# Token parts, first weight pieces and output weights moved ahead at the seam between attention and FFN

## The chip, the cores and the metric

The kernel runs on one core of a Trainium2 chip. The metric is the device time in microseconds (us) of one execution; with several runs of a kernel, their median. Engines are called as the profile calls them: PE (TensorE, matmuls), PEld (its weight loads), DVE (VectorE), ACT (ScalarE), POOL (GpSimd), and SP (SyncE, which issues every DMA here). Each engine works through its own list of instructions in order and waits on semaphores for the others.

## The reference

A transformer block with both branches fed by one layer norm:

```
xn  = layernorm(x)                       # x: 1 x 2048 x 512, f32
qkv = xn @ w_qkv.T                       # 16 heads of 32
p   = softmax(causal(q k^T / sqrt(32)))
a   = (p v) @ w_o.T
gate, up = xn @ Wg.T, xn @ Wu.T          # Wg, Wu: 4096 x 512, Wd: 512 x 4096
inter    = gelu_tanh(gate) * up          # weights: 4-bit codes times a scale for 32 of them
out = x + a + inter @ Wd.T
```

## The kernel before

The order of the instructions on every engine is the order in which the program writes them (`manual_schedule`); pools of tiles decide which earlier reader a new tile has to wait for.

**Attention.** The 2048 tokens are four blocks `b` of 512, taken in `ORDER = (1, 2, 3, 0)`; the normalized tokens stand transposed in `xnT[b]`, 128 features by 512 tokens for each `k` of 4. Heads go in eight pairs `p`. A first part normalizes the tokens and makes values, queries and keys; its tiles for `x`, `wv` and `xn` live in pools of their own. A pair takes 40 steps, one for each block of queries `qb` and tile of keys `kt`. In a step `score_cols` starts two score tiles in PSUM with the negated row maxima (L281), `add_scores` adds the products (L296), `exponentials` turns them into probabilities on ACT (L310; on the diagonal, the last four `kt` of a block, L316 to L320 and POOL's affine select L321), and `attend` multiplies the step before by the values and by ones for the row sums (L344). When a block of queries is full, `keep_attention` copies the result on ACT (L363) and the sums on DVE (L364), and four `normalize_attention` follow, one for each step: a reciprocal on DVE (L372) and a product on POOL (L374). The last two pairs, with no row maxima left to find, run together in one loop of 40 steps. Score tiles rotate through three PSUM banks for each of two pools, and one step takes two of each.

**Output projection.** It starts with the loads of `w_o` (`wo`, L714) into buffers of the pool `gu`, and 16 loads of `x` into accumulators `acc` (L719), between which `fetch` loads three weight pieces. Then come 16 tiles of 128 tokens `n`, each with four matmuls into a PSUM bank `po` (L726), and DVE adds it to `acc` (L733). Eight banks take turns, here and in the FFN.

**Token parts.** The FFN's products are made from parts of 12 bits. For each `xnT[b][:, k]`, `token_rest` makes on DVE `high` (tile `highx`, L692), on POOL the rest `low` (tile `lm`, L693), and, one tile of the projection later, on DVE `mixed` (L695) and on ACT the rescaled `low` (L698). `token_high` makes `xh` on DVE (L703), in the buffer of an attention output that the projection has read. In the projection there is one `token_rest` for each tile `n`, 16 in all.

**Weight pieces.** `begin_piece` decodes 128 x 512 codes: five instructions on DVE (L582 to L596) and two on POOL (L602 or L608). `end_piece` cuts them: `high` on DVE (L620), two on ACT (L632, L633), two on POOL (L634, L635). For the down weights `raise_low` comes later on ACT (L645). Three pieces are made within the projection, and the fourth within the first unit of the FFN.

**FFN.** 128 units (g, j, b). A unit has 16 matmuls for gate and up (`high_and_low`, L765), each sum scaled in place on ACT (L772), four more for each (`mixed`, L778), the gelu on ACT (L797), the product `inter` on DVE (L801), and its parts (L805, L808, L809). The down product of a unit, `down`, is a generator which the next unit drives through `finish`: between gelu and up's `mixed` it makes the third part (L816), eight matmuls (L826) and four scalings on ACT (L833), and at the unit's end four matmuls (L838) and the sums into `acc` (L847).

Of the kernel before, what the change touches and what calls it, by code (L numbers as in the profile page):

```python
# [45 lines left out]
P = 128  # L46
# [29 lines left out]
def block_kernel(  # L76
# [11 lines left out]

    late = ctx.enter_context(tc.tile_pool(name="late", bufs=1, side="right"))
# [13 lines left out]
    with (  # L103
# [3 lines left out]
        tc.tile_pool(name="wa", bufs=2) as wa,  # L107
        tc.tile_pool(name="vals", bufs=1) as vals,
        tc.tile_pool(name="qk", bufs=10) as qkp,
# [4 lines left out]
        tc.tile_pool(name="clip", bufs=2) as clipp,  # L114
        tc.tile_pool(name="ps_s", bufs=3, space=PSUM) as ps_s,
# [261 lines left out]
        with (  # L377
            tc.tile_pool(name="x", bufs=1) as xp,
            tc.tile_pool(name="xn", bufs=2) as xnp,
        ):  # L380
            xs = []
            for t in range(NT):
                xt = xp.tile([P, H], F32, tag=f"x{t % 8}", name=f"x{t}")
                nc.sync.dma_start(out=xt, in_=x[t * P : (t + 1) * P, :])
                xs.append(xt)
                if t == 3:
                    wqk[0] = load_qk(0)
                    wv = xp.tile([P, NK, H], F32, tag="wv", name="wv")
                    nc.sync.dma_start(out=wv, in_=w_v.rearrange("p (k o) -> p k o", k=NK))
            wqk[1] = load_qk(1)  # L390
            mvs, rstds = {}, {}

            def statistics(b, first=0, n=4):
                key = f"{b}_{first}"
                mv = small.tile([P, n, 2], F32, tag="mv", name=f"mv{key}")
                for i in range(n):
                    st = small.tile([P, 6], F32, tag="st", name=f"st{key}_{i}")
                    nc.vector.bn_stats(st, xs[4 * b + first + i])
                    nc.vector.bn_aggr(mv[:, i, :], st)
                ve = small.tile([P, n], F32, tag="ve", name=f"ve{key}")  # L400
                nc.vector.tensor_scalar(ve, mv[:, :, 1], EPS, None, ALU.add)
                sd = small.tile([P, n], F32, tag="sd", name=f"sd{key}")
                nc.scalar.activation(sd, ve, AF.Sqrt)

                q = small.tile([P, n], F32, tag="q", name=f"q{key}")
                nc.vector.reciprocal(q, sd)
                nc.vector.tensor_tensor(q, q, ve, ALU.mult)
                nc.vector.tensor_tensor(q, q, sd, ALU.add)
                nc.vector.tensor_scalar(q, q, 0.5, None, ALU.mult)
                rstd = small.tile([P, n], F32, tag="rstd", name=f"rstd{key}")  # L410
                nc.vector.reciprocal(rstd, q)
                for i in range(n):
                    mvs[b, first + i], rstds[b, first + i] = mv[:, i, 0:1], rstd[:, i : i + 1]

            xns = {}

            def normalize(b, i):
                xn = xnp.tile([P, NK, 8, 16], F32, tag="xn", name=f"xn{b}_{i}")
                nc.vector.tensor_scalar(
                    xn,  # L420
                    xs[4 * b + i].rearrange("p (b r k) -> p k r b", b=16, r=8),
                    mvs[b, i],
                    rstds[b, i],
                    ALU.subtract,
                    ALU.mult,
                )
                xns[b, i] = xn

            def flip(b, i):

                bank = i % 2 if b == 0 else b < 3
                pt = ps_m.tile([P, TB], F32, tag=f"m{int(bank)}", name=f"ptx{b}_{i}")
                xn = xns.pop((b, i))
                for k in range(NK):
                    nc.tensor.transpose(  # L435
                        pt[:, k * P : (k + 1) * P], xn[:, k].rearrange("p r b -> p (r b)"), ident
                    )
                nc.scalar.copy(
                    xnT[b][:, :, i * P : (i + 1) * P],
                    pt.rearrange("p (k t) -> p k t", k=NK),  # L440
                )

            def value_halves(t):
                ps = ps_m.tile([P, H], F32, tag="m0", name=f"ps_v{t}")
                for k in range(NK):
                    nc.tensor.matmul(  # L446
                        ps,
                        lhsT=xnT[t // 4][:, k, (t % 4) * P : (t % 4 + 1) * P],
                        rhs=wv[:, k, :],
                        start=(k == 0),  # L450
                        stop=(k == NK - 1),
                    )
                    if k == 1:
                        yield
                nc.scalar.copy(v[t // 4][:, t % 4, :], ps)
                yield

            for i in range(4):
                if i % 2 == 0:
                    statistics(0, i, 2)  # L460
                normalize(0, i)
                flip(0, i)

            later = [(1, b, which) for b in range(NTB) for which in range(2)]
            for b in range(NTB):
                n = first[b]
                if b + 1 < NTB:
                    statistics(b + 1)
                    normalize(b + 1, 0)
                project(0, b, 0)  # L470
                project(0, b, 1)
                for i in range(4):
                    if b + 1 < NTB:
                        flip(b + 1, i)
                    full_width = [value_halves(4 * b + i)] * 2
                    if b >= 2:
                        full_width += [project_halves(*later.pop(0))] * 2
                    for j in range(b + 1):
                        rows_when_due()
                        tiles = [score_rows(0, n, ps_s), score_rows(1, n, ps_t)]  # L480
                        for p in range(2):
                            maxima(p, n, tiles[p])
                        if j == 0 and i < 3 and b + 1 < NTB:
                            normalize(b + 1, i + 1)
                        n += 1
                        for _ in range(-(-len(full_width) // (b + 1 - j))):
                            next(full_width.pop(0))
# [4 lines left out]
        for m in range((NP - 2) * STEPS):  # L492
# [25 lines left out]
            if og + 2 < NOG and own == 20:  # L518
                wqk[og + 2] = load_qk(og + 2)
        for n in range(STEPS):  # L520
            rows_when_due(joint=True)
            two = [score_cols(NP - 2, n, ps_t), score_cols(NP - 1, n, ps_s)]
            for i in range(2):
                add_scores(NP - 2 + i, n, two[i])
            for _ in range(2):
                attend(*pending.pop(0))
            for i in range(2):
                pending.append((NP - 2 + i, n, exponentials(NP - 2 + i, n, two[i])))
            while full:
                keep_attention()  # L530
            if invert:
                normalize_attention()
        while pending:
            attend(*pending.pop(0))
# [6 lines left out]
    lmp = ctx.enter_context(tc.tile_pool(name="lm", bufs=1, reuse_waits="tile"))  # L541
    accp = ctx.enter_context(tc.tile_pool(name="acc", bufs=1, reuse_waits="tile"))
    stage = ctx.enter_context(tc.tile_pool(name="stage", bufs=3, reuse_waits="tile"))
    tp = ctx.enter_context(tc.tile_pool(name="deq", bufs=2, reuse_waits="tile"))
    gup = ctx.enter_context(tc.tile_pool(name="gu", bufs=4, reuse_waits="tile"))
# [132 lines left out]


    lm = [lmp.tile([P, 2, NK, TB], F32R, tag=f"lm{b}", name=f"lm{b}") for b in range(NTB)]  # L680
    xh = {}

    def end(rest):
        if rest is not None:
            for _ in rest:
                pass

    def token_rest(b, k):

        x, low, mixed = xnT[b][:, k], lm[b][:, 0, k], lm[b][:, 1, k]  # L690
        high = tp.tile([P, TB], F32, tag="high", name=f"highx{b}_{k}")
        nc.vector.tensor_scalar(high.bitcast(I32), x.bitcast(I32), HIGH, None, ALU.bitwise_and)  # L692
        nc.gpsimd.tensor_tensor(low, x, high, ALU.subtract)  # L693
        yield
        nc.vector.scalar_tensor_tensor(  # L695
            mixed, high, SPLIT, low.bitcast(F32), ALU.mult, ALU.subtract
        )
        nc.scalar.activation(low, low.bitcast(F32), AF.Copy, scale=1.0 / SPLIT)  # L698
# [8 lines left out]
    with tc.manual_schedule():  # L707
# [10 lines left out]
        for n, t in enumerate(order):  # L718
            nc.sync.dma_start(out=acc[t], in_=x[t * P : (t + 1) * P, :])  # L719
            if n in (1, 2, 3):  # L720
                fetch()
        tokens = None
        for n, t in enumerate(order):
# [21 lines left out]
            if n in (3, 6, 9):  # L745
                begin_piece()
# [164 lines left out]
```

## Time and profile before

| | us |
|---|---|
| runs shown | 2002.93, 2003.64, 2005.29 |
| their median | 2003.64 |
| the profiled execution | 2003.17 |
| its span | 2001.5 |
| PE busy | 1954.4 |
| DVE busy | 1316.7 |
| ACT busy | 1105.0 |
| POOL busy | 730.8 |
| last two pairs of heads begin, about | 735 |
| first matmul of the output projection | 855.88 |
| its last one ends | 912.2 |
| third unit of the FFN begins | 940.95 |

All times of the profile come from one execution and are counted from the start of its span; the time of that execution is 1.67 us longer than the span. Rows of a stage give, after its length, the busy time of PE, PEld, DVE, ACT and POOL with the number of instructions, then the granted clock of PE (1.00 is full speed), the busy share of the DMA engines and GB/s. Rows of a timeline give start, length, engine, line, operation, output and input, and in brackets the idle time ahead of it with what ended it. A row of the chain gives start, length and what ran. A row of the waits reads "who <- for whom: us in total, times, the longest".

### The profile page before, as it was taken

To read this page: it belongs to the slowest core of one execution; us is meant where nothing else is said; L and a number is where in the kernel's file an instruction comes from. 1 tells how busy PE (TensorE), PEld (TensorE's weight loads), DVE (VectorE), ACT (ScalarE), POOL (GpSimd) and SP (SyncE) were. 2 spreads that over 40 slices of the span, in tenths; PEclk is the share of its full clock that TensorE was granted. 3 is DMA by queue.
4 is the path that set the end of the run, shared out by engine and by line. 5 is a ranking of instruction groups with operands and counts; after the bars stand their busy time and mean duration, and the time that the engine had idled before them with its cause. 6 is when DMAs were issued, how large, how long until landed. Compare 5 with 4: busy or idle time off the path is not lost.

```text
span 2001.5 us, 30992 instructions
## 1 busy us (share of the span) xinstructions
PE 1954.4 (98%) x11072; PEld 1162.7 (58%) x11072; DVE 1316.7 (66%) x2642; ACT 1105.0 (55%) x2360; POOL 730.8 (37%) x892
## 2 busy tenths in 40 slices
PE   7999999999999999997999999999999999999998
PEld 3433233333333322245888888888888888888886
DVE  5657665646565661178776767676767676767674
ACT  2112664546455667724666666666666666666664
POOL 1000110202111112155555555555555555555551
PEclk9999999999999999998999999999999999999999
DMA  3000000000000000030000000000000000000002
GB/s 126 0 11 11 1 2 1 1 1 1 1 1 1 1 2 1 1 128 17 24 22 19 22 20 21 20 22 19 22 19 22 19 21 20 22 19 22 19 6 84
DMA packets 54955, 39.79 MB, mean 20 GB/s; under 512 B 14736, under 2 KB 47504, under 8 KB 54672
## 3 DMA queue, kind: packets, MB, share of 16 engines
q1 hardware_dynamic: 54800, 37.81, 6.4%
q8 instruction: 87, 1.43, 0.3%
q14 instruction: 68, 0.56, 0.1%
HBM read 33.55 MB, written 4.19 MB: 19 GB/s over the span
## 4 chain that ended last, share of the span: by engine, by line
PE 93%; DVE 2%; ACT 2%; issue 1%; POOL 1%; DMA 0%; POOLq 0%; DVEq 0%; ACTq 0%
PE gu L765 23%; PE av L344 12%; PE pd L826 12%; PE gu L778 12%; PE ps_s L207 9%; PE ps_qk L163 6%; PE pd L838 6%; PE ps_t L281 4%; PE ps_t L296 3%; PE ps_v L446 3%; ACT prob L310 1%; PE po L726 1%; POOL lm L693 1%; PE pm L262 1%; PE ptx L435 0%
## 5 line engine op out<-in xcount | busy, mean ns | idle before, releaser
L765 PE MATMUL gu<-xh,gu 128*128 128x512 f32 x1024 | 403.3, 394 | 0.0
L765 PE MATMUL gu<-lm,gu 128*128 128x512 f32 x1024 | 399.9, 390 | 0.0
L231 DVE TENSOR_REDUCE tops<-ps_s 128x1 f32<-128x512 f32 x384 | 243.6, 681 | 157.5 <-PE ps_s L207 137.2
L847 DVE SCALAR_TENSOR_TENSOR acc<-pd,acc 128x512 f32<-128x512 f32 x512 | 316.7, 679 | 0.7 <-PE pd L838 0.7
L344 PE MATMUL av<-prob,v 128*32 128x512 f32 (+3 forms) x1280 | 288.8, 539 | 3.7 <-DVE sums L364 2.8
L310 ACT ACTIVATE prob<-ps_t 128x512 f32<-128x512 f32 x384 | 205.8, 597 | 154.5 <-PE ps_t L296 153.2
L207 PE MATMUL ps_s<-qk,qk 32*128 32x512 f32 (+3 forms) x1280 | 291.1, 576 | 0.0
L778 PE MATMUL gu<-lm,gu 128*128 128x512 f32 x1024 | 279.5, 395 | 10.3 <-ACT gu L772 10.3
L344 PE MATMUL av<-prob,ones 128*32 128x512 f32 (+3 forms) x1280 | 288.8, 539 | 0.0
L809 POOL TENSOR_TENSOR parts<-inter,hi 128x512 fp32r<-128x512 f32 x128 | 171.7, 1341 | 269.6 <-DVE hi L805 267.5
L801 DVE SCALAR_TENSOR_TENSOR inter<-gu,gate 128x512 f32<-128x512 f32 x128 | 88.5, 692 | 271.1 <-PE gu L778 266.8
L833 ACT ACTIVATE pd<-pd 128x512 f32<-128x512 f32 x512 | 263.2, 581 | 1.9 <-PE pd L826 1.9
L296 PE MATMUL ps_t<-qk,qk 32*128 32x512 f32 (+3 forms) x1280 | 263.6, 535 | 0.0
L826 PE MATMUL pd<-wd,parts 128*128 128x512 f32 x1024 | 260.5, 396 | 2.4 <-ACT parts L808 1.1
L772 ACT ACTIVATE gu<-gu 128x512 f32<-128x512 f32 x256 | 148.5, 580 | 182.8 <-PE gu L765 182.8
L778 PEld LDWEIGHTS gu<-lm,gu 128*128 128x128 f32 x1024 | 192.9, 188 | 56.6 <-ACT gu L772 10.7
L826 PEld LDWEIGHTS pd<-wd,parts 128*128 128x128 f32 x1024 | 192.6, 188 | 49.5 <-ACT parts L808 1.5
L765 PEld LDWEIGHTS gu<-xh,gu 128*128 128x128 f32 x1024 | 192.7, 188 | 46.5 <-ACT lm L698 0.2
L765 PEld LDWEIGHTS gu<-lm,gu 128*128 128x128 f32 x1024 | 191.9, 187 | 43.1 <-issue 0.2
L321 POOL TENSOR_SCALAR_AFFINE_SELECT prob<-prob 128x256 f32<-128x256 f32 x128 | 52.0, 407 | 430.8 <-ACT prob L320 384.2
L226 DVE CUSTOM_DVE_ANT_0 ps_s<-ps_s,mask_qk 128x128 f32<-128x128 f32 (+3 forms) x256 | 120.7, 516 | 101.6 <-PE ps_t L296 55.8
L808 ACT CAST parts<-hi 128x512 fp32r<-128x512 f32 x128 | 79.8, 623 | 172.8 <-DVE hi L805 172.8
(86 smaller groups left out, 2688.5 us busy)
## 6 DMA issues: line engine op xcount, KB each, us to landing
pk<-packed SPq DMA_DIRECT2D x96, 128.0 KB, 2.1
sc<-scales SPq DMA_DIRECT2D x512, 8.0 KB, 1.6
x<-x SPq DMA_DIRECT2D x16, 256.0 KB, 3.9
acc<-x SPq DMA_DIRECT2D x16, 256.0 KB, 4.7
sc<-scales SPq DMA_DIRECT2D x256, 16.0 KB, 1.7
out<-acc SPq DMA_DIRECT2D x16, 256.0 KB, 2.2
wqk<-w_qk SPq DMA_DIRECT2D x4, 512.0 KB, 3.7
wv<-w_v SPq DMA_DIRECT2D x1, 1024.0 KB, 7.3
```

The costliest lines, as they stand in the source:

```text
L207: nc.tensor.matmul(ps[:, :w], lhsT=qT[p // 2, qb][rows, i * P : (i + 1) * P], rhs=kT[p // 2, c][rows, :w], start=True, stop=True,)
L231: nc.vector.tensor_reduce(top, ps[:, :w], AX.X, ALU.max)
L296: nc.tensor.matmul(ps[:, c0:], lhsT=kT[p // 2, kt // 4][rows, (kt % 4) * P : (kt % 4 + 1) * P], rhs=qT[p // 2, qb][rows, c0:], start=False ...
L310: nc.scalar.activation(prob[:, h, :], ps, AF.Exp)
L344: nc.tensor.matmul(av[D * h : D * (h + 1), c0:], lhsT=v[kt // 4][:, kt % 4, D * head : D * (head + 1)] if h < 2 else ones, rhs=prob[:, h % ...
L765: nc.tensor.matmul(ps, lhsT=parts[:, i, k], rhs=mov, start=(k == 0 and i == 0), stop=(k == NK - 1 and i == 1),)
L772: nc.scalar.activation(ps, ps, AF.Copy, scale=HIGH_SCALE)
L778: nc.tensor.matmul(ps, lhsT=gu[g, m, j][:, 2, k], rhs=lm[b][:, 1, k], start=False, stop=(k == NK - 1), skip_group_check=True,)
L809: nc.gpsimd.tensor_tensor(parts[:, 1], inter, high, ALU.subtract)
L826: nc.tensor.matmul(po, lhsT=parts[:, part, i * P : (i + 1) * P], rhs=w[:, part], start=(part == 0), stop=(part == 1),)
L833: nc.scalar.activation(po, po, AF.Copy, scale=HIGH_SCALE)
L847: nc.vector.scalar_tensor_tensor(acc[t], po, SUM_SCALE, acc[t], ALU.mult, ALU.add)
```

## The change

The diff does seven things.

1. The tiles of the first part (`x`, `wv`, `xn`) move to a pool `turns` that stays open, `wv` as four tiles with a load each. The code between loses one level of indentation and is otherwise the same.
2. In the loop of the last two pairs, at even `kt` off the diagonal, one `token_rest` begins; its second half follows one step later. Eight are made so, for the blocks `ORDER[:2]`; `lm` goes to buffers of `turns`, `high` to one of the pool `qk`.
3. `wo` is loaded in the loop of the pairs before, in the two buffers of the projection weights `wqk`, once these have been read.
4. The projection makes the other eight token parts, in its first eight tiles, and all four first pieces, begun at n = 1, 4, 9, 12 and cut at 3, 6, 11, 14. The first unit of the FFN no longer begins a piece.
5. The loads of `acc` come in `ORDER`, and `fetch` after the sixth, tenth and fourteenth of them.
6. One gelu of a single column (`warm`) stands at the head of the projection, so that ACT loads its table there.
7. `down` has one more stop, ahead of its eight matmuls. All units but the last drive past it at once; in the last unit the eight matmuls of the unit before come after up's `mixed`.

```diff
+    turns = ctx.enter_context(tc.tile_pool(name="turns", bufs=1, side="right"))
+    def turn_tile(i, name, dtype=F32, shape=(P, TB)):
+        return turns.tile(list(shape), dtype, tag=f"turn{i}", name=name)
+    wa = ctx.enter_context(tc.tile_pool(name="wa", bufs=2))
...
-                    wv = xp.tile([P, NK, H], F32, tag="wv", name="wv")
-                    nc.sync.dma_start(out=wv, in_=w_v.rearrange("p (k o) -> p k o", k=NK))
+                wv = [turn_tile(8 + k, f"wv{k}") for k in range(NK)]
+                for k in range(NK):
+                    nc.sync.dma_start(out=wv[k], in_=w_v[:, k * H : (k + 1) * H])
...
+            if og + 2 == NOG and own == max(places_own) + 1:
+                wo = []
+                for i in range(0, NOG, 2):
+                    t = wa.tile([P, 2, H], F32, tag="wqk", name=f"wo{i}")
+                    for k in range(2):
+                        nc.sync.dma_start(out=t[:, k], in_=w_o[i + k])
+                        wo.append(t[:, k])
+        lm = {}
+        def token_rest(b, k, high):
+            xk, (low, mixed) = xnT[b][:, k], lm[b, k]
+            nc.vector.tensor_scalar(
+                high.bitcast(I32), xk.bitcast(I32), HIGH, None, ALU.bitwise_and
+            )
+            nc.gpsimd.tensor_tensor(low, xk, high, ALU.subtract)
+            yield
+            nc.vector.scalar_tensor_tensor(
+                mixed, high, SPLIT, low.bitcast(F32), ALU.mult, ALU.subtract
+            )
+            nc.scalar.activation(low, low.bitcast(F32), AF.Copy, scale=1.0 / SPLIT)
+            yield
+        early = [(i, k) for i in range(2) for k in range(NK)]
+        rest = iter(())
         for n in range(STEPS):
...
             if invert:
                 normalize_attention()
+            next(rest, None)
+            qb, kt = steps[n]
+            if early and kt < 4 * qb and kt % 2 == 0:
+                i, k = early.pop(0)
+                b = ORDER[i]
+                lm[b, k] = [
+                    turn_tile(8 * i + 2 * k + part, f"lm{b}_{k}_{part}", F32R)
+                    for part in range(2)
+                ]
+                rest = token_rest(b, k, qkp.tile([P, TB], F32, tag=f"qk{k % 2}", name=f"hx{b}_{k}"))
+                next(rest)
...
-        wo = []
-        for og in range(0, NOG, 2):
-            t = gup.tile([P, 3, NK, P], F32, tag="gu", name=f"wo{og}")
-            for i in range(2):
-                wo.append(t[:, i].rearrange("p k o -> p (k o)"))
-                nc.sync.dma_start(out=wo[og + i], in_=w_o[og + i])
+        warm = tp.tile([P, 1], F32, tag="warm", name="warm")
+        nc.gpsimd.memset(warm, 0.0)
+        nc.scalar.activation(warm, warm, AF.Gelu_apprx_tanh)
...
-            if n in (1, 2, 3):
+            if n in (5, 9, 13):
                 fetch()
-        tokens = None
+        begin, finish = (1, 4, 9, 12), (3, 6, 11, 14)
+        tokens = iter(())
         for n, t in enumerate(order):
...
             nc.vector.tensor_tensor(acc[t], acc[t], po, ALU.add)
-            end(tokens)
-            tokens = token_rest(t // 4, t % 4)
-            next(tokens)
+            next(tokens, None)
+            if n < 8:
+                b, k = ORDER[2 + n // NK], n % NK
+                tokens = token_rest(
+                    b, k, tp.tile([P, TB], F32, tag="high", name=f"highx{b}_{k}")
+                )
+                next(tokens)
             if n >= 4:
                 token_high(ORDER[n // 4 - 1], n % 4)
...
-            if n in (3, 6, 9):
+            if n in begin:
                 begin_piece()
-            if n in (5, 8, 12):
+            if n in finish:
                 end_piece()
-        end(tokens)
+        raise_low()
...
-            if (g, j, b) == (0, 0, ORDER[0]):
-                begin_piece()
...
+            last = (g, j, b) == (NG - 1, NC - 1, ORDER[-1])
             next(finish, None)
+            if not last:
+                next(finish, None)
             mixed(g, 1, j, b, up_sum)
...
             end_piece()
+            if last:
+                next(finish, None)
             next(finish, None)
...
-            if (g, j, b) == (0, 0, ORDER[0]):
-                raise_low()
+            yield
             w = wd[g, j // 2][:, j % 2]
```

The line numbers of the changed program are higher: what stands at L281, L296 and L310 before is at L288, L303 and L317 after, L726 at L753, L772 at L803. `token_rest` is at L539 to L547, the loads of `wo` at L530.

## The prediction

> **What bounds the kernel now.** I read the page first, then the busy time by stage, then the chain of waits and the waits through the seam between attention and FFN, then each engine's timeline there.
>
> ```profile
> PE 1954.4 (98%) x11072; PEld 1162.7 (58%) x11072; DVE 1316.7 (66%) x2642; ACT 1105.0 (55%) x2360; POOL 730.8 (37%) x892
> ```
>
> TensorE is the bound, so only its idle or slowed microseconds are to be had. Where are they? By stage (us, PE, PEld, DVE, ACT, POOL busy, clock):
>
> ```profile
> 735.00:855.00 120.00, 111.53 (x1140) 33.47 (x1136) 23.99 (x35) 91.29 (x251) 23.30 (x58) 1.00 0.01 3
> 855.00:913.00 58.00, 57.12 (x130) 25.25 (x131) 46.02 (x69) 9.85 (x16) 32.70 (x27) 0.97 0.34 111
> 913.00:927.00 14.00, 3.73 (x16) 2.73 (x16) 11.73 (x18) 5.00 (x9) 8.12 (x6) 0.70 0.00 0
> 927.00:941.00 14.00, 12.97 (x45) 10.04 (x46) 8.85 (x17) 7.92 (x14) 7.14 (x7) 0.82 0.11 30
> 941.00:1941.00 1000.00, 1000.00 (x4318) 809.88 (x4317) 740.87 (x1386) 622.41 (x1172) 555.39 (x484) 1.00 0.08 20
> ```
>
> The FFN is full for 1000 us, one unit (g, j, b) each 8.34 us. The hole is 913 to 927, at a clock of 0.70, and the stretch behind it is still at 0.82. The chain there:
>
> ```profile
> 853.15 2.60 DMA wo<-w_o
> 855.88 15.68 PE po L726 x32
> ...
> 925.57 0.61 ACT wd L645
> 926.18 0.49 ACT gu L772
> 926.72 3.78 PE gu L778 x8
> 930.50 4.50 PE gu L765 x16
> ...
> 940.95 3.69 PE gu L765 x16
> ```
>
> Two waits: the output projection for its weights, and the first unit's second half for ScalarE. The waits of 852 to 930 say why ScalarE was late:
>
> ```profile
> ACT lm L698 <- DVE lm L695: 53.1, 16, 12.2
> PE gu L778 <- ACT gu L772: 10.3, 1, 10.3
> PE po L726 <- DMA wo<-w_o: 2.7, 1, 2.7
> ```
>
> ScalarE's eviction L772 of unit 0 is queued behind the sixteenth lm (L698, 925.03), and VectorE, which makes the token parts, is the late one: its list of 16 times (acc add, highx, lm, xh) and three weight pieces runs from 861 to 927, while TensorE's sixteen po are done at 912.2.
>
> **The change, part by part.**
>
> *Output projection, start.* The wo loads leave. In the built program the first po waits then for the last sums copy (L364), which frees its PSUM bank; it ends at 854.58. So po starts at 854.65 instead of 855.88: gain 1.2. SP's queue loses four issues (1.75 us) at its head: six acc loads, then pk and sc of piece 0, acc and pieces in turn. acc now lies where it waits for the last exponential (852.2) and lands about 4.7 later (median of its row), at 857; VectorE is in its last reciprocals to 858.0 and the first po is done at 858.1, so no loss. Piece 0 lands near 862 (six acc issues of 0.42, eight sc in 5.1), its decode comes near 863.
>
> *Clock.* The rows of that gap:
>
> ```profile
> 856.00:858.00 2.00, 2.00 (x4) 0.52 (x4) 2.00 (x3) 0.00 (x0) 1.06 (x3) 0.77 0.90 253
> 858.00:860.00 2.00, 2.00 (x4) 0.90 (x4) 0.00 (x0) 0.00 (x0) 0.45 (x1) 0.50 1.00 352
> ```
>
> The half clock lasted 3.4 us, from 857.1 to 860.5, and cost po 1.7: it took 56.3 (855.88 to 912.2) where 128 records of 0.427 are 54.6. The Trainium skill (TensorE: Matmul & The Clock Gate, "HAM oscillation") wants no idle gap above some 3.4 us. This case disagrees: a gap of 2.8 was enough, as the busy share inside one window of 3.4 us counts (1.2 busy here; 1.95 around 845 drew nothing). By the gap rule the 1.6 us that remain are safe and the 1.7 is gained; by the trace a window over 851.3 to 854.7 has only 1.2 busy, so it comes back if the window falls so, about one time in three. I take it as gained, with +1.7 in the range.
>
> *Output projection, VectorE.* Eight token parts leave it: per part highx, lm on VectorE, 1.64 on POOL (L693), 0.63 on ScalarE. A fourth weight piece enters (decode 2.4, high 0.42 to 1.5). I laid VectorE's list against po n, done at 854.65+3.41(n+1), with the rhythms of this trace: 4.3 for an n with a decode, 6.8 with decode and contention, 2.8 to 4.2 else. It falls behind in n=4 to 8 (n=4 ends 878.7 against po at 871.7, n=7 at 889.7 against 881.9), where eight PSUM banks cover a lag up to eight po (27 us); from n=8 on no token part is left, and it is level at n=13 (904.2 against 902.4). Piece 3 is cut at n=14: high at 907.4, POOL 1.3 and 1.6 to 910.3, raise_low on ScalarE to 911. TensorE ends po at 909.25, the gate half of unit 0 at 911.1, the up half at 912.95. So L772 is no longer waited for. The Gelu table load (1.28) moves to where ScalarE is idle; it was not on the chain. The four last xh (2.4) end at 912.9, before the first gelu at 913.9 that takes their buffers.
>
> *Sum of the seam.* Unit 0 has no down part before it: 3.69+0.93+0.93 = 5.55, so unit 1 starts at 914.8 and unit 2 at 923.1, against 940.95 in the chain: **gain 17.8**. (Its parts: 1.2 start, 1.7 clock, 10.3 wait, 2.9 half clock behind it, 1.7 smaller waits of units 0 and 1.)
>
> *Attention's last two pairs.* Eight token parts enter steps that are off the diagonal, at even kt; the second half of a part (lm on VectorE and ScalarE) stands one step on. VectorE has room (24 of 120 us), ScalarE less: four exponentials take 2.06 of a step of 3.04, and one lm 0.53 more. But ScalarE works in order, and lm waits for VectorE, which waits for POOL. At a block's start VectorE itself begins late, behind the sums copies:
>
> ```profile
> 762.18 1.42 DVE L364 COPY sums<-av 64x512 f32<-64x512 f32 x2 [15.71 <-ACT aT L363]
> 763.63 3.39 DVE L372 RECIPROCAL sums<-sums 128x128 f32<-128x128 f32 x4
> ...
> 764.73 0.46 POOL L374 TENSOR_TENSOR aT<-aT,sums 128x128 f32<-128x128 f32 x1 [5.03 <-DVE sums L372]
> ...
> 762.70 2.06 ACT L310 ACTIVATE prob<-ps_t 128x512 f32<-128x512 f32 x4
> 766.13 2.06 ACT L310 ACTIVATE prob<-ps_t 128x512 f32<-128x512 f32 x4 [1.36 <-PE ps_t L296]
> ```
>
> Put in the part: first reciprocal to 764.5, high 0.42 to 764.9, POOL's aT to 765.2, its subtraction 1.27 to 766.5, lm on VectorE 0.6 to 767.1, lm on ScalarE to 767.7. The next exponentials, at 766.13 now, start 1.55 late; the third of them frees the bank that the next step's L281 wants, with 0.2 to spare: TensorE waits 1.35. The same at the start of block 3 (sums at 797.08): 1.35. At block 1 only one copy is ahead: 0.8 late, 0.6 lost. TensorE cannot catch up at 100%: **loss 3.3**. The five other parts start when VectorE runs ahead; their lm is ready when ScalarE comes to it. Bounds: 0 if the slack at the banks is larger than I read; 3.2 more if high takes 1.5 instead of 0.42 each time. For that the Trainium skill (SBUF — State Buffer, the shared port pair) has a rule against this move: VectorE in a two-port mode, or with two SBUF inputs, and GpSimd exclude each other for a whole instruction, and this puts eight subtractions of 1.3 beside reciprocals and affine selects. The trace has both values (highx 420 ns at the median, 1506 at most); at a block's start POOL is idle when high begins (its aT comes 0.3 after), so I take 0.42; by the rule at its worst the loss is 6.5.
>
> *Elsewhere.* wv in four loads puts three SP issues (1.4) ahead of x4 to x7; their statistics begin at 12.7 and the first use of the result on TensorE is 26.6: the row's 8 us of slack hide it. The wo loads stand on an idle SP near 600 us. The order inside all FFN units but the last is unchanged. In the last, up's second half goes ahead of the previous unit's down half: 1.87 earlier, but ScalarE must first cast the last parts (to 1990.9) and then scale four pd (2.05), so the last down half starts at 1993.25 instead of 1993.62: gain 0.4 (0 to 1).
>
> *Sum.* -17.8+3.3-0.4 = -14.9. It is made against the profiled execution (2003.17; span 2001.5 and 1.67 around it); the median shown is 2003.64, 0.47 above. So **1988.7**.
>
> **Rivals.**
> 1. *The block starts cost nothing* (the banks have more slack). For: ScalarE is idle 0.98 per step. Against: the fourth L281 of these steps already waits for an exponential. 2003.64-18.2 = 1985.4. Chance 0.17.
> 2. *VectorE or POOL stay late in the projection, or the clock drops, or high meets POOL*: one or two of +1.7, +3.2, +3 (piece 3 late into unit 0): 1990.5 to 1995. Chance 0.22.
> 3. *The stall returns whole*: the fourth piece, now inside, with its raise_low ahead of L772, is as late as the sixteenth lm was. Then 10.3 and 2.9 of clock stay: -17.8+13.2+3.3-0.4 = -1.7, 2001.9, no change. It decides if VectorE ends n=14 after some 920, 12 us later than my list. Chance 0.03.
> 4. *Slower*: each of the eight lm, not only the three at block starts, holds ScalarE behind POOL for a whole step of TensorE, 3.04: 24.3 against the gain of 18.2, 2009.7. It decides from 2.3 per part. POOL's queue would have to be late in the middle of a block, where it has only 0.46 of aT per step. Chance 0.05.
>
> My forecast has 0.53. A measurement of this kernel tells 0.2% (4 us) from no change. The range runs from rival 1 with some room to the middle of rival 2: 1984.8 to 1993.5. Faster 0.92 (forecast, rivals 1 and 2), same 0.03, slower 0.05.
>
> **What would show it.** Right: no wo in the chain; po from 854.6 plus the attention's loss; no L803 wait of TensorE behind po; unit 2 some 14.5 earlier than 940.95; after each sums copy at kt=0 ScalarE's lm waits for VectorE, and a step two further on waits over 1 us. The forecast is wrong if TensorE idles more than 3 us between po and unit 1, or if the steps of the last two pairs have grown in the middle of a block.

## The result, and the profile after

| | before | after |
|---|---|---|
| median, us | 2004.94 (2002.93 to 2005.84, 8 runs) | 1999.15 (1996.45 to 1999.57, 8 runs) |
| profiled execution, its span | 2003.17, 2001.5 | 1999.17, 1997.4 |

The ratio after to before is 0.9972, 95% interval 0.9961 to 0.9983. The change made the kernel faster by 0.3%: by 5.8 us of the medians and 4.0 of the two profiled executions. The forecast was a gain of 14.9, that is 1988.7 us with a range of 1984.8 to 1993.5: the measured median lies above the range. So the question of this study is where 11 us of the gain expected for the profiled execution went.

First the profile's row of engines, then the same stages as before. Columns: length, PE, PEld, DVE, ACT and POOL busy (instructions), clock, DMA share, GB/s.

```profile
PE 1960.7 (98%) x11072; PEld 1162.0 (58%) x11072; DVE 1311.8 (66%) x2642; ACT 1105.3 (55%) x2361; POOL 727.4 (36%) x893
```

```profile
...
855.00:913.00 58.00, 55.84 (x171) 24.41 (x164) 44.20 (x69) 14.49 (x31) 31.82 (x33) 0.97 0.32 98
913.00:927.00 14.00, 14.00 (x53) 9.70 (x52) 8.10 (x15) 5.19 (x9) 3.87 (x3) 1.00 0.05 11
...
941.00:1941.00 1000.00, 1000.00 (x4297) 806.08 (x4296) 736.27 (x1377) 618.78 (x1166) 552.28 (x482) 1.00 0.08 20
```

The hole at 913 to 927 is gone (PE busy 14.00 of 14.00 at full clock, where it was 3.73 at 0.70). But PE is busy 6.3 us longer in all, for the same 11072 matmuls, and in the 1000 us of the FFN it does 4297 of them where it did 4318: at 100% busy and clock 1.00 in both. The chain shows the seam (start, length, what ran):

```profile
859.60 0.71 DVE sums L371
...
860.35 56.77 PE po L753 x128
917.12 3.73 PE gu L796 x16
920.85 1.92 PE gu L809 x8
922.77 3.73 PE gu L796 x16
...
931.16 3.71 PE gu L796 x16
...
939.53 3.71 PE gu L796 x16
```

No load of `wo` stands ahead of po, which waits for the last sums copy instead, and there is no wait for ScalarE between po and unit 1. The `gu L796` rows are units 0, 1, 2 and 3: unit 2 begins at 931.16 where it began at 940.95. In this table of the two traces (starts and ends of TensorE's own records) each stretch stands by itself, so that each difference is booked once:

| us | before | after | difference | forecast |
|---|---|---|---|---|
| last av of attention ends | 853.18 | 858.89 | +5.7 | +3.3 |
| from there to the first po | 2.70 | 1.45 | -1.25 | -1.2 |
| first po to unit 0 | 56.3 | 56.2 | -0.1 | -1.7 |
| unit 0 to unit 2 | 28.6 | 14.45 | -14.15 | -14.9 |
| unit 2 to unit 127 | 1042.5 | 1047.7 | **+5.2** | 0 |
| unit 127 to the span's end | 18.17 | 18.73 | +0.56 | -0.4 |

The +5.7 in attention is 4.4 of stalls at block starts, 1.6 of half clock (a stretch in which the granted clock was 0.50), and a start that lay 0.3 earlier in this execution. The seam did nearly what was forecast. Five microseconds were lost where the change alters no instruction at all: in the 125 units between. The rest of the miss is in attention, in the clock and at the end.

### The profile page after: what moved, and what is told of

Read it like the earlier page. It is cut to its first block, busy times and chain, and to the rows that moved or that the text cites. A ratio compares the mean times of both kernels' runs of the same rounds, so it can differ in the third digit from the quotient of the medians.

```text
span 1997.4 us, 30985 instructions
## 1 busy us (share of the span) xinstructions
PE 1960.7 (98%) x11072; PEld 1162.0 (58%) x11072; DVE 1311.8 (66%) x2642; ACT 1105.3 (55%) x2361; POOL 727.4 (36%) x893
## 4 chain that ended last, share of the span: by engine, by line
PE 95%; ACT 2%; DVE 1%; issue 1%; POOL 0%; DMA 0%; DVEq 0%; POOLq 0%; ACTq 0%
PE gu L796 24%; PE av L351 12%; PE gu L809 12%; PE pd L859 12%; PE ps_s L214 9%; PE ps_qk L170 6%; PE pd L871 6%; PE ps_t L288 4%; PE ps_t L303 3%; PE ps_v L450 3%; PE po L753 3%; ACT prob L317 1%; PE pm L269 1%; PE ptx L439 0%; DVE sums L371 0%
## 5 line engine op out<-in xcount | busy, mean ns | idle before, releaser
L796 PE MATMUL gu<-xh,gu 128*128 128x512 f32 x1024 | 403.9, 394 | 0.0
L796 PE MATMUL gu<-lm,gu 128*128 128x512 f32 x1024 | 403.7, 394 | 0.0
L317 ACT ACTIVATE prob<-ps_t 128x512 f32<-128x512 f32 x384 | 205.8, 596 | 148.0 <-PE ps_t L303 146.6
L303 PE MATMUL ps_t<-qk,qk 32*128 32x512 f32 (+3 forms) x1280 | 264.2, 535 | 0.0
L803 ACT ACTIVATE gu<-gu 128x512 f32<-128x512 f32 x256 | 148.7, 581 | 188.2 <-PE gu L796 188.2
L796 PEld LDWEIGHTS gu<-lm,gu 128*128 128x128 f32 x1024 | 191.9, 187 | 46.6 <-POOL wd L677 0.2
L796 PEld LDWEIGHTS gu<-xh,gu 128*128 128x128 f32 x1024 | 192.0, 188 | 45.7 <-ACT wd L676 0.2
```

Source lines behind the costliest of these rows:

```text
L303: nc.tensor.matmul(ps[:, c0:], lhsT=kT[p // 2, kt // 4][rows, (kt % 4) * P : (kt % 4 + 1) * P], rhs=qT[p // 2, qb][rows, c0:], start=False ...
L317: nc.scalar.activation(prob[:, h, :], ps, AF.Exp)
L796: nc.tensor.matmul(ps, lhsT=parts[:, i, k], rhs=mov, start=(k == 0 and i == 0), stop=(k == NK - 1 and i == 1),)
L803: nc.scalar.activation(ps, ps, AF.Copy, scale=HIGH_SCALE)
```

## Experiments

Two theories stood for the FFN. **Placement:** the change moved tiles in SBUF, and a matmul's rate depends on where its operands lie. One operand of a matmul is loaded as weights, the other streams past it: `xh` and `lm` are streamed past `gu` in gate and up, and in the down product `wd` is streamed past the parts of `inter`. In the built program of before, `gu`, `wd` and `lm` begin at 128 bytes modulo 512 of a partition (the remainder of the address after division by 512), `xh` and the parts at 480. In after, the tile `warm` takes 32 bytes in each of the two buffers of its pool, below `gu` and `wd`, and shifts both by 64 bytes (to 192); and the `lm` of blocks 1 and 2, now in buffers of `turns`, begin at 480. The diff also puts some pools in another order (`acc` now stands behind `stage`, `deq` and `gu`), which the list of seven things leaves out; that moves `gu` and `wd` by a multiple of 512 only, and run 5, which keeps it, has before's FFN. **Rival:** order or traffic, that is, a wait or a DMA whose cost the trace spreads over the units. In favour of the rival is that no wait is shown; against it, that the units differ by block `b` and are steady for 1000 us. In ORDER (blocks 1, 2, 3, 0) they take 8.389, 8.400, 8.364 and 8.373 us, and took 8.34 each before. In the profile's costliest groups (busy us, mean ns of one | idle ahead) the matmuls that stream `lm` have grown from 390 to 394 ns over all 1024 of their group, while those that stream `xh` stood at 394 already. After:

```profile
L796 PE MATMUL gu<-xh,gu 128*128 128x512 f32 x1024 | 403.9, 394 | 0.0
L796 PE MATMUL gu<-lm,gu 128*128 128x512 f32 x1024 | 403.7, 394 | 0.0
```

Before:

```profile
L765 PE MATMUL gu<-xh,gu 128*128 128x512 f32 x1024 | 403.3, 394 | 0.0
L765 PE MATMUL gu<-lm,gu 128*128 128x512 f32 x1024 | 399.9, 390 | 0.0
```

These means are a hint and no more, since the profile models where a matmul ends (run 7 has the same 394 for `lm` with units almost as short as before's). The starts are firm: the sixteen matmuls that gate and up begin with take 3.685 us of a unit in before and 3.705 to 3.730 in after, which is most of what the unit has grown by.

**1. The weights' 64 bytes taken back.** `warm` becomes a column of a tile that exists anyway.

```diff
-        warm = tp.tile([P, 1], F32, tag="warm", name="warm")
+        warm = tp.tile([P, TB], F32, tag="high", name="warm")[:, :1]
```

> The changed kernel with the one column for the early gelu taken from a buffer that exists (high) instead of a tile of its own, so that the weight parts gu and wd lie 64 bytes lower, as far from a multiple of 2048 as in the kernel before. Layout theory, weights' place: units of the FFN with b = 3 and 0 return from 8.36 and 8.37 to 8.34 us, units with b = 1 and 2 from 8.39 and 8.40 to about 8.36; the span falls by some 3. Layout theory, only the place of lm counts: nothing changes (8.39, 8.40, 8.36, 8.37). Rival, contention (DMA queues or POOL load the SBUF differently): nothing changes.

Measured: 1996.32 (one run). Units 8.385, 8.38, 8.335, 8.34: the blocks 3 and 0, whose `lm` had stayed in place, are back at before's 8.34, and the blocks 1 and 2 are not. From unit 2 to unit 127 it is 1044.97, 2.7 shorter than in after. So taking back 64 bytes of address of the weights takes back half of the loss, and the other half stays with the `lm` in `turns`.

**2. Addresses of lm and xh.** On top of 1, unused tiles were to put `lm` of blocks 1 and 2 back.

```diff
     turns = ctx.enter_context(tc.tile_pool(name="turns", bufs=1, side="right"))
+    pad = turns.tile([P, 40], F32, tag="pad_a", name="pad_a")
...
+    pads = ctx.enter_context(tc.tile_pool(name="pads", bufs=1, side="right"))
+    pad_b = pads.tile([P, 88], F32, tag="pad_b", name="pad_b")
```

> As the kernel with the shared gelu column, and two unused tiles of 160 and 352 bytes on the right side, so that lm of blocks 1 and 2 lies at a multiple of 64 bytes (and 128 past a multiple of 512), as in the kernel before, with xh and parts where they are relative to 512. Layout theory: all units at 8.34 us, the span 5 us below that of the changed kernel, about 1994 in time. If the distance to the attention outputs or something else than the layout counts: units with b = 1 and 2 stay above 8.34.

Measured: 1996.63, ratio 0.9962 (0.9948 to 0.9976); units 8.385, 8.38, 8.335, 8.34, as in 1. The experiment missed its aim: the tile in the same pool did not push the others, so `lm` still began at 480, and only `xh` and the parts had moved, by exactly 512 bytes. What it says is therefore another thing: a shift of `xh` (streamed) and of the parts (loaded as weights) by 512 changes nothing. The question of `lm` went to run 5.

**3. The 64 bytes alone, in before.** Two unused columns in the same pool, nothing else.

```diff
+        for i in range(2):
+            nc.gpsimd.memset(tp.tile([P, 1], F32, tag="warm", name=f"warm{i}"), 0.0)
         wo = []
```

> The kernel before with nothing but one unused column in each of two buffers of the decoding pool: gu and wd move up by 64 bytes, lm, xh and parts stay. Layout theory, weights' place: all units become 0.02 to 0.03 us longer, 8.36 to 8.37, the time 3 us longer than before. If only the place of lm counts, or contention: 8.34, no change (0 to 0.5 us).

Measured: 2007.88 against 2004.18 of before, ratio 1.0020 (1.0011 to 1.0029). All units take 8.373, unit 2 to unit 127 1046.66 (+4.15). Two consecutive units in the chain of this kernel, and then of before:

```profile
994.67 3.71 PE gu L767 x16
...
1003.05 3.71 PE gu L767 x16
```

```profile
1007.67 3.69 PE gu L765 x16
1016.01 3.69 PE gu L765 x16
```

8.38 from start to start against 8.34; of the 33 ns by which a unit is longer, 29 lie in the first sixteen matmuls of gate and up. A shift of 64 bytes costs before 3.7 us with no instruction of the FFN changed. (The decoding tiles of that pool shift too, but TensorE reads none of them.) That is shown without any other part of the change, and it rules out the rival for this half. The two shifts do not simply add: from unit 2 to unit 127 the weights' alone costs 4.15 (this run), that of `lm` alone 2.5 (run 1 against before), and both together 5.2 (after).

**4. No token part at a block's first step.** The slots of the loop of the last two pairs are kept, but for `kt` = 0.

```diff
-            if early and kt < 4 * qb and kt % 2 == 0:
+            if early and 0 < kt < 4 * qb and kt % 2 == 0:
```

> The changed kernel with no token part begun at kt = 0 of a block of queries: the eight slots are then kt = 2 of block 1, 2 to 6 of block 2, 2 to 8 of block 3. Theory, ScalarE is held behind a part whose VectorE half is late behind the sums copies: the three stalls of 1.0, 1.7 and 1.7 us of TensorE go, the last two pairs end 4.3 earlier, the time falls by 4 (the phase of the clock windows can add or take 1.7). Rival, the added work on ScalarE or POOL as such takes the time: the loss stays at 3 to 4.3 and only moves two steps on.

Measured: 1994.53, ratio 0.9953 (0.9938 to 0.9968), which is 9.7 below before in the same runs, where after gained 5.8. In this execution the first step of the last two pairs begins 1.81 us later than in before, and up to a half clock in the last block every other step lies 1.5 to 1.8 later too: no stall is left of the three, which took 0.97, 1.69 and 1.71 in after. Unit 2 to unit 127 stays at 1047.69. ScalarE at the start of block 2, in after and then here (start, length, engine, line, operation, output and input; in brackets the idle time ahead):

```profile
763.41 2.07 ACT L317 ACTIVATE prob<-ps_t 128x512 f32<-128x512 f32 x4
768.04 0.63 ACT L547 ACTIVATE lm<-lm 128x512 fp32r<-128x512 f32 x1 [2.56 <-DVE lm L544]
768.58 2.04 ACT L317 ACTIVATE prob<-ps_t 128x512 f32<-128x512 f32 x4
```

```profile
764.51 2.06 ACT L317 ACTIVATE prob<-ps_t 128x512 f32<-128x512 f32 x4
767.86 2.06 ACT L317 ACTIVATE prob<-ps_t 128x512 f32<-128x512 f32 x4 [1.29 <-PE ps_t L303]
...
772.83 0.65 ACT L547 ACTIVATE lm<-lm 128x512 fp32r<-128x512 f32 x1
```

In after ScalarE stands 2.56 us in front of the `lm` that VectorE has not written, with the exponentials queued behind it. Here the exponentials wait only for TensorE, and the `lm` comes in two steps later with no wait. The mechanism of the forecast's attention term is shown, and it was avoidable.

**5. lm moved.** On top of 1, one unused pool ahead of `turns` and one behind it; `lm` of the blocks 1 and 2 now begins at 128 modulo 512.

```diff
+    pads_a = ctx.enter_context(tc.tile_pool(name="pads_a", bufs=1, side="right"))
+    pad_a = pads_a.tile([P, 88], F32, tag="pad_a", name="pad_a")
     turns = ctx.enter_context(tc.tile_pool(name="turns", bufs=1, side="right"))
...
+    pads_b = ctx.enter_context(tc.tile_pool(name="pads_b", bufs=1, side="right"))
+    pad_b = pads_b.tile([P, 40], F32, tag="pad_b", name="pad_b")
```

> The changed kernel with the shared gelu column, and an unused tile of 352 bytes above the pool turns and one of 160 below it, so that now lm of blocks 1 and 2 itself moves by 352 bytes, to a multiple of 64 and 128 past a multiple of 512 as in the kernel before; xh moves by 512 as in the run before. (In that run only xh had moved: the pad came to lie below lm.) Layout theory: units with b = 1 and 2 fall from 8.385 and 8.38 to 8.34 us, the FFN's 125 units from 1045.0 to 1042.5. Rival, the distance of lm from xh or the separate tiles count: they stay.

Measured: 1992.72, ratio 0.9935 (0.9921 to 0.9949). All units 8.34, unit 2 to unit 127 1042.50: before's FFN is whole again. The profile's row for the matmuls that stream `lm` is back at 390 ns:

```profile
L802 PE MATMUL gu<-lm,gu 128*128 128x512 f32 x1024 | 399.4, 390 | 0.0
```

This kernel has every instruction of after's FFN, in the same order and with the same transfers, so the rival falls for the other half too: runs 1, 3 and 5 together show that placement carries the FFN's 5.2 us.

**6. All of it.** On top of 5: the slots of run 4; the last unit in the order of before; and the FFN's PSUM pool with waits for each tile, so that the first po waits for its own bank and not for the last sums copy.

```diff
-            if early and kt < 4 * qb and kt % 2 == 0:
+            if early and 0 < kt < 4 * qb and kt % 2 == 0:
...
-    ps_f = ctx.enter_context(tc.tile_pool(name="ps_f", bufs=8, space=PSUM))
+    ps_f = ctx.enter_context(tc.tile_pool(name="ps_f", bufs=8, space=PSUM, reuse_waits="tile"))
...
-            last = (g, j, b) == (NG - 1, NC - 1, ORDER[-1])
+            last = False
```

> All that the runs point to: the aligned kernel, no part at kt = 0, the last unit of the FFN in the order of before, and the PSUM banks of the second half waiting for their own tiles alone, so that the first po no longer waits for the last sums copy. Theory: against the changed kernel 5.2 from the units' length, 4.3 from the attention, 0.5 from the tail, 1.4 from the gap ahead of po, and up to 3.4 where the half clock no longer falls: 1984 to 1988. Rival, gains that hide each other: more than 1991.

Measured: 1987.43 (1984.27 to 1988.05), ratio 0.9906 (0.9892 to 0.9919); profiled 1984.6. This beats both kernels: 18.4 us under before in the same runs. Its chain at the seam:

```profile
852.57 0.43 PE av L357 x8
853.00 55.13 PE po L759 x128
908.13 3.69 PE gu L802 x16
911.82 1.99 PE gu L815 x8
913.81 3.68 PE gu L802 x16
...
922.14 3.00 PE gu L802 x13
```

po follows the last av without a gap and takes 54.64 (852.93 to 907.57): the full-clock figure. From the start of unit 127 to the last accumulated group it is 12.49, as before's 12.51; after had 12.81.

**7 and 8. How far the placement rule reaches.** Both on before. Run 7 moves `xh` and the parts by 32 bytes, from 480 to 448 modulo 512, so that they begin at a multiple of 64; run 8 moves `gu` and `wd` by 512.

```diff
+    pads_a = ctx.enter_context(tc.tile_pool(name="pads_a", bufs=1, side="right"))
+    pad_a = pads_a.tile([P, 8], F32, tag="pad_a", name="pad_a")
```

> The kernel before with one unused tile of 32 bytes at the top of the right side: xh and the parts of inter move from 32 past a multiple of 64 to a multiple of 64, lm, gu and wd stay. Layout theory, a row of 64 bytes is what counts: the units become shorter than 8.34 us (8.30 or less). Layout theory, the distance between what is streamed and the weights counts: the unit changes either way by 0.02 to 0.06. No layout effect of these tiles: 8.34.

```diff
+        for i in range(2):
+            nc.gpsimd.memset(tp.tile([P, 64], F32, tag="warm", name=f"warm{i}"), 0.0)
```

> The kernel before with 256 bytes unused in each of two buffers of the decoding pool: gu and wd move up by 512 bytes, lm, xh and parts stay. Layout theory with a period of 512 or less: units at 8.34 us, no change. With a longer period (2048 or more): another length, up to 8.40.

Measured (one run each, with before at 2005.83): run 7 2004.47, units 8.347; run 8 2005.81, units 8.34. Run 7's row for `lm`, which did not move:

```profile
L768 PE MATMUL gu<-lm,gu 128*128 128x512 f32 x1024 | 403.8, 394 | 0.0
```

`xh` at a multiple of 64 is not faster (0.006 a unit slower), so nothing here supports the idea that a row of 64 bytes decides. A shift of the weights by 512 costs nothing, as one of `xh` did in run 2; that the pattern repeats at 512 rests on these two shifts, and for `lm` it was not tested.

**9. The token parts back in the projection.** Run 6 with all 16 parts made beside po, everything else kept.

```diff
-        early = [(i, k) for i in range(2) for k in range(NK)]
+        early = []
...
-            if n < 8:
-                b, k = ORDER[2 + n // NK], n % NK
+            if n < 16:
+                b, k = ORDER[n // NK], n % NK
```

> The combined kernel with all sixteen token parts made within the output projection again, one for each tile, and none beside the last two pairs; wo early, four pieces within, aligned tiles as in the combined kernel. Theory of the prediction, the token parts make VectorE late: its list ends some 13 to 16 later than po, the first unit waits for ScalarE again, 10 us or more, with a window or two of half clock behind it; unit 2 begins about 15 to 18 later than in the combined kernel, time 2001 to 2006. Rival, the early weights and the other order of pieces are what helped: less than 5 lost, below 1992.

Measured: 2001.1, ratio to before 0.9979 (0.9970 to 0.9989). Unit 0 to unit 2 takes 29.35 where run 6 has 14.41. Its waits (who <- for whom: us in total, times, the longest):

```profile
PE gu L821 <- ACT gu L815: 13.3, 1, 13.3
...
ACT lm L553 <- DVE lm L550: 44.0, 15, 6.3
```

The wait of before is back, 13.3 long, with a half clock over and behind it (917.9 to 931.5). The moved token parts carry the whole gain of the seam, 14.9; earlier weights and wo without them don't.

**10. The weight pieces as before.** Run 6 with three pieces in the projection and the fourth begun in unit 0.

```diff
-        begin, finish = (1, 4, 9, 12), (3, 6, 11, 14)
+        begin, finish = (3, 6, 9), (5, 8, 12)
...
+            if (g, j, b) == (0, 0, ORDER[0]):
+                begin_piece()
```

> The combined kernel with the weight pieces as before: three begun at n = 3, 6, 9 and cut at 5, 8, 12, the fourth begun in the first unit of the FFN. Theory of the prediction, with eight token parts gone VectorE has room for either: unit 0 to 2 take the same, the time within 1.5 of the combined kernel. Rival, the fourth piece in the first unit delays inter and so the down part: 2 to 4 us lost.

Measured: 1988.06 (1986.63 to 1989.32), ratio 0.9914 (0.9899 to 0.9928). Unit 0 to unit 2 takes 16.59, 2.2 more than run 6. The chain shows the first down product waiting for the late piece:

```profile
920.77 1.60 POOL wd L684
...
922.40 0.64 ACT wd L694
...
923.08 1.90 PE pd L868 x7
```

I had put it at 1.5 at most and the rival at 2 to 4, and the trace sides with the rival. The two medians differ by only 0.6, within the spread of the runs: that this part of the change is worth anything in the median is not shown.

## Why the prediction was wrong, point by point

**"The order inside all FFN units but the last is unchanged", so each unit stays at 8.34: the step that failed.** The sentence is true and the conclusion isn't. 125 units became 5.2 us longer, 35% of the forecast gain, because a one-column tile and a new pool moved the operands. Run 3 shows the shift of the weights alone (+4.15 from unit 2 to unit 127), runs 1 and 5 take the whole away in two steps (-2.7 and -2.5). The rivals looked for a late engine or a dropped clock; none allowed for a matmul that is slower with no wait in the trace. The addresses of both kernels were there to be compared, though nothing in the trace of before told what a shift costs.

**The clock: 3.2 us, by a choice that fell on the wrong side and by bad luck.** The prediction set the rule of the Trainium skill (TensorE: Matmul & The Clock Gate, "HAM oscillation": no idle gap above some 3.4 us) against the trace, held the trace to be right, and then booked the gain that goes with the rule. Rows of after, same columns as the stages: two within a half clock, then the 3.41 us ahead of each.

```profile
850.00:852.00 2.00, 2.00 (x12) 0.56 (x11) 1.97 (x3) 2.00 (x9) 0.43 (x2) 0.50 0.00 0
860.00:862.00 2.00, 1.66 (x2) 0.84 (x3) 1.97 (x3) 1.07 (x2) 0.45 (x1) 0.53 0.95 305
...
846.48:849.89 3.41, 1.22 (x15) 0.41 (x14) 0.85 (x2) 3.36 (x11) 0.81 (x2) 1.00 0.00 0
856.72:860.13 3.41, 1.49 (x24) 0.47 (x24) 1.23 (x2) 2.83 (x7) 1.71 (x6) 1.00 0.32 91
```

There are two half clocks of 3.41 us. The one from 860.13 follows a gap of 1.45 (po takes 56.2, not 54.6: the 1.7 isn't gained). The one from 849.89 follows a dip in TensorE's work at the start of the last block: sixteen av took 3.61 where before had 1.93, and the prediction had no such term (1.6). By the cited rule no gap here was long enough; the rows disagree with the page, as in before.

But the change did not make that dip. Before has it too and drew no half clock, and run 5 drew none from dip or gap. First before's dip, then both in run 5:

```profile
843.41:846.82 3.41, 1.95 (x21) 0.82 (x24) 1.76 (x3) 3.36 (x12) 0.59 (x2) 1.00 0.00 0
```

```profile
851.72:855.14 3.42, 2.11 (x21) 0.84 (x24) 1.92 (x3) 3.37 (x13) 0.51 (x2) 1.00 0.00 0
...
858.55:861.96 3.41, 2.08 (x36) 0.58 (x32) 0.69 (x1) 2.76 (x9) 2.11 (x6) 1.00 0.14 47
```

In every trace the half clocks begin a multiple of 3.41 us apart (849.89 and 860.13 are three apart), as if on a grid, and the rows are stretches of the grid of their trace. In these rows, a stretch with TensorE 1.22 or 1.49 us busy is followed by one at half clock, and stretches with 1.95 to 2.11 are not. That fits the prediction's own reading, the busy share inside one window, but it is no clean rule: in run 5 a half clock from 810.76 follows a stretch with 2.45 busy. How the grid falls is luck: of twelve traces six have a half clock at the last block (after and runs 1, 3, 4, 6 and 10, of which run 3 has before's attention), and of the five with this gap ahead of po four have one in po (after and runs 1, 2 and 4), where the prediction allowed one time in three. Run 6 has the dip and no gap: one half clock is left, from 843.93, and its po runs at 54.64. The medians do not separate these 3.2 us; only the traces do.

**"Loss 3.3" in attention: right mechanism, sized 1.1 too small.** Block starts of the last two pairs cost 0.97, 1.69 and 1.71, together 4.4, against 0.6, 1.35 and 1.35. No step in the middle of a block grew, as forecast. The terms of the sum, at block 2:

```profile
764.27 0.95 DVE L379 RECIPROCAL sums<-sums 128x128 f32<-128x128 f32 x1
765.14 0.36 DVE L539 TENSOR_SCALAR hx<-xnT 128x512 int32<-128x512 int32 x1
...
765.78 1.27 POOL L542 TENSOR_TENSOR lm<-xnT,hx 128x512 fp32r<-128x512 f32 x1
...
767.00 0.46 POOL L381 TENSOR_TENSOR aT<-aT,sums 128x128 f32<-128x128 f32 x1
...
767.08 0.93 DVE L544 SCALAR_TENSOR_TENSOR lm<-hx,lm 128x512 fp32r<-128x512 f32 x1 [0.72 <-POOL lm L542]
```

The reciprocal (0.87 from its start to that of `high`, for 0.85), `high` at 0.36 and POOL at 1.27 were as assumed. The mis-sized term is VectorE's second `lm`: 0.93 where I took 0.6 from an undisturbed one. POOL's product for `aT` runs beside it; in run 6 the parts with no such product beside them take 0.69. That makes 0.3 of the 0.35 or so by which each stall is longer; the meeting of VectorE and GpSimd that the prediction weighed for `high` seems to have come at `lm`. Run 4 shows that the whole 4.4 goes with those three parts.

**The seam: right.** The gap ahead of po shrank by 1.25 for 1.2; unit 0 to unit 2 is 14.45 long, -14.15 for -14.9. From the first matmul to unit 2 I had counted 13.85. Of the 0.6 more, 0.4 is that the first matmul of unit 0 begins 0.63 ahead of the second instead of 0.23, as it does in before and in run 6; the longer units make 0.04 (run 6 takes 14.41), and the rest is not traced. TensorE no longer waits for ScalarE; the waits of 852 to 935 have it the other way about:

```profile
ACT lm L547 <- DVE lm L544: 29.6, 8, 9.3
...
ACT gu L803 <- PE gu L796: 4.1, 4, 1.3
```

Run 9 (+14.9 without the moved parts) shows what carries it, and rival 3, in which the fourth piece would be late, did not come.

**"Gain 0.4" at the tail: wrong in sign.** From unit 127 to the last accumulated group it takes 12.81, where before took 12.51, and to the end of the span it is 0.56 longer. Timeline of TensorE and ScalarE there:

```profile
1987.22 1.96 PE L871 MATMUL pd<-wd,parts 128*128 128x512 f32 x4 [0.92 <-ACT pd L866]
...
1986.07 0.62 ACT L840 CAST parts<-hi 128x512 fp32r<-128x512 f32 x1 [1.86 <-DVE hi L837]
1986.59 2.04 ACT L866 ACTIVATE pd<-pd 128x512 f32<-128x512 f32 x4
```

The eight matmuls that went behind up's `mixed` no longer fill the time in which ScalarE casts and scales: TensorE waits 0.92 for the four pd. Run 6, with before's order and otherwise moved work, has 12.49. The other 0.26, behind the last group, stands in run 6 too and is not traced.

Added up: 5.2 of placement, 3.2 of clock, 1.1 of attention's stalls, 0.95 of the tail and 0.75 of the seam, less the 0.3 by which attention began earlier, are 10.9, the gap between the forecast 14.9 and the profiled 4.0. None of the rivals described this. Rival 2 named the clock, but had no term for placement and so ended below the measured time; rival 3 has the nearest number, 2001.9, by a late fourth piece that did not occur. Neither of the prediction's two signs of being wrong came: TensorE did not idle between po and unit 1, and no step grew in the middle of a block.

## What to carry to other kernels

When a change opens, closes or enlarges any buffer, compare the addresses of the operands of the inner matmuls before and after: a shift that no instruction shows took back 5.2 of the 14.15 us that were gained at the seam, and an unused tile can undo it. Work given to an in-order engine at a moment when its supplier is behind holds up everything queued there, so put it a step or two later, where the supplier is ahead. A gap of 1.5 us ahead of a stream of matmuls can cost more than itself: in four of five traces here it drew a half clock of 3.4.

## What the hardware showed unexpectedly

A matmul at 100% busy and full granted clock has no fixed rate: with `gu` and `wd` shifted by 64 bytes in SBUF a unit of the FFN went from 8.34 to 8.373 us (run 3), with `lm` at 480 instead of 128 bytes modulo 512 to 8.38 (run 1), while shifts of 512 changed nothing (`xh` and the parts in run 2, `gu` and `wd` in run 8) and one of 32 in `xh` and the parts added 0.006 (run 7). Which pair of addresses collides, and in what, stays open: these runs give a few points of a table and no rule. A half clock came already after gaps of 1.45 to 2.9 us and then lasted 3.41 us (after the waits of 10 us and more, 13.65 in before and run 9 and 10.24 in runs 3, 7 and 8), but not always: the same 1.45 drew none in run 5.
